# Another order of the first loads and first matmuls in a gated cross-attention and expert kernel

## The chip, the cores and the metric

The kernel runs on one core of a Trainium2 chip. The metric is the device time of one execution in microseconds. Besides the unprofiled runs there is one execution taken by the profiler; its lines give start times and durations on each engine: TensorE (PE, with its weight loads as PEld), VectorE (DVE), ScalarE (ACT), GpSimd (POOL), and SyncE (SP), which here only issues DMAs.

## What is computed

A batch of 4 sequences x of 512 tokens and width 256 attends to a context of 1601 tokens and width 192, and then goes through a layer of experts. Everything is float32.

```python
def block(x, y):                      # cross-attention, 16 heads of 16
    q = (x @ Wq + bq).reshape(B, N, 16, 16)
    k = (y @ Wk + bk).reshape(B, M, 16, 16)
    v = (y @ Wv + bv).reshape(B, M, 16, 16)
    attn = softmax(einsum("bnhd,bmhd->bhnm", q, k) / 4)
    out = einsum("bhnm,bmhd->bnhd", attn, v).reshape(B, N, 256)
    return relu(out @ W1 + b1) @ W2 + b2
x = x + tanh(g_xattn) * block(layernorm(x), ctx)
x = x + tanh(g_ffn) * experts(layernorm(x))   # one shared, two of eight routed by sigmoid scores
```

## The kernel before

**Layout.** The 16 heads are worked on in four groups of four (`G` = 4 groups, `HPG` = 4 heads), each head in 32 of the 128 partitions, of which 16 hold values. `wk_t` holds the K weights of all heads without gaps, so one product (`make_k`, lines 301 to 315) makes K of 8 heads for one of four chunks (`NCH`) of 401 or 398 context tokens; a bias row is the 97th row of the second half of the weights and meets a row of ones in the context. Each product is two matmul calls (`c` = 0, 1), and each call is two passes in float32. The result goes to PSUM, ACT copies it into `kd`, and `spread` (lines 317 to 323) then moves the rows of four heads by four DMAs, one for each head, into one of three tiles `ks` with 32 partitions a head. `make_v` (line 328) makes V of one tile of 128 context tokens (there are 13, `NKT`); it is kept in one of 15 tiles `vs`, whose unused columns hold zeros and one column of ones.

**Main loop.** The scheduler keeps the order as written for TensorE, ACT, DVE and SP. For each pair of a batch and a group, 13 steps run: in each, scores of one group (line 416, exponents on ACT at 425), the attention times V (`add_values`, 437), and already the maxima of the next group (`maximum`, 357, reduced by DVE at 368). Other work (Q, K, V of later batches, the MLP of earlier ones) is put beside given steps in the table `late` by `put`. A step that gets such work of a larger kind goes into the set `large` and does its attention-times-V product in one piece, others in two halves. A second phase, after line 697, does the experts, with pieces of the shared expert placed by `fill` between the last MLP, the last layer norm and the router.

**Start.** `first_loads` (lines 177 to 192) issues DMAs on two queues, SP's and ACT's. K weights come first on SP, then the first context chunk, x of batch 0 and the other chunks; ACT issues the K bias row, the Q bias and the V bias. Line 181 writes the bias row element by element, since the biases lie in columns in memory. A DMA is given one of eight semaphores in turn, so the issuing of a ninth waits for the first to land. ACT then packs `wk_slots` into `wk_t` (lines 660 to 665), in two copies; the second takes in the bias row. Next, in the order of lines 666 to 694: statistics of x on DVE (`stats1`), K chunks 0 and 1, the reciprocal square root of the variance by four Newton steps (`rstd_of`, lines 234 to 250), the normalised x (`apply`, line 254), its transposes (`make_xnT`), K chunks 2 and 3, the spreads for groups 0 and 1, the remaining loads (`other_loads`: gates, x of batches 1 to 3, MLP weights), Q of groups 0 and 1, and the first V tile. A loop over 13 slices then finds the maxima of group 0: four matmuls, four reductions by DVE, and one further product of V or K in each slice; the K parts of the second eight heads stand in slices 3 to 6. Three V tiles are left to the first steps of the main loop. POOL and DVE fill constant tiles at the very start (lines 157 to 166).

`rstd_of` runs on DVE for batch 0 at the start and for batch 3 at the end of attention (line 775), on POOL for the others.

Of the kernel before, what the change touches and what calls it, by code (L numbers as in the profile page):

```python
# [8 lines left out]
FP = mybir.dt.float32  # L9
AF = mybir.ActivationFunctionType  # L10
ALU = mybir.AluOpType
# [3 lines left out]
P = 128  # L15
EPS = 1e-5
HD = 16
# [8 lines left out]
def kernel(  # L26
# [43 lines left out]
    nc = tc.nc  # L70
    B, D, M = ctxT.shape
    NT, H = x.shape
    S = NT // B
# [4 lines left out]
    KC = D // 2  # L78
    NKT = -(-M // P)
    NCH = 4  # L80
    CH = -(-M // NCH)
    chunks = [(c * CH, min(CH, M - c * CH)) for c in range(NCH)]
# [44 lines left out]
    gt = const.tile([P, 2], FP, name="gt")  # L127
# [16 lines left out]
    sp1 = xattn.enter_context(tc.tile_pool(name="sp1", bufs=1, side="right"))  # L144
    esp = xattn.enter_context(tc.tile_pool(name="esp", bufs=10, side="right"))
    wq_t = sp1.tile([P, 2, G * P], FP, name="wq_t")
# [14 lines left out]
    for t in ks:  # L161
        nc.gpsimd.memset(t, 1.0)
    nc.gpsimd.memset(neg, 0.0)
    for t in vs:
        nc.gpsimd.memset(t, 0.0)
        nc.gpsimd.memset(t[:, :, HD : HD + 1], 1.0)

    def load_ctx(b, parts=((0, M),)):
        for o, n in parts:
            nc.sync.dma_start(  # L170
                out=ctx_t[:KC, :, o : o + n],
                in_=ctxT[b].rearrange("(c p) m -> p c m", p=KC)[:, :, o : o + n],
            )
# [2 lines left out]

    def first_loads():

        nc.sync.dma_start(out=wk_slots[:KC], in_=wk.rearrange("(c p) n -> p c n", p=KC))
        nc.scalar.dma_start(  # L180
            out=wk_slots[KC : KC + 1, 1, :].rearrange("o (g p) -> o g p", p=P),
            in_=bk.rearrange("(o p) g -> o g p", o=1),
        )
        load_ctx(0, chunks[:1])
        load_x(0)
        load_ctx(0, chunks[1:])
        nc.scalar.dma_start(out=bq_t, in_=bq)
        nc.scalar.dma_start(
            out=wv_t[KC : KC + 1, 1, :], in_=bv.rearrange("(o n) -> o n", o=1)
        )  # L190
        nc.sync.dma_start(out=wq_t, in_=wq.rearrange("(c p) n -> p c n", p=P))
        nc.sync.dma_start(out=wv_t[:KC], in_=wv.rearrange("(c p) n -> p c n", p=KC))

    def other_loads():
        nc.sync.dma_start(out=gt, in_=gates.partition_broadcast(P))
        for b in range(1, B):
            load_x(b)
        for h in range(NH):
            nc.sync.dma_start(
                out=w1_t[h * HD % P : h * HD % P + HD, h * HD // P, :],  # L200
                in_=w1[h * HS : h * HS + HD, :],
            )
        nc.sync.dma_start(out=b1_t, in_=b1)
        nc.sync.dma_start(out=w2_t, in_=w2.rearrange("(c p) n -> p c n", p=P))
        nc.sync.dma_start(out=b2_t, in_=b2.partition_broadcast(P))
        nc.sync.dma_start(out=rb_t, in_=rb.partition_broadcast(P))
        nc.sync.dma_start(out=ord_t, in_=order.partition_broadcast(P))
        nc.sync.dma_start(out=wr_t, in_=wrT.rearrange("(c p) e -> p c e", p=P))
# [25 lines left out]
    def rstd_of(b, mv, rstd, engine):  # L234

        var = p2.tile([P, NTB], FP, tag="var")
        nc.vector.tensor_scalar(var, mv[:, rows(b), 1], EPS, None, ALU.add)
        first = p2.tile([P, NTB], I32, tag="first")
        nc.vector.tensor_scalar(first, var.bitcast(I32), 1, None, ALU.arith_shift_right)  # L239
        nc.vector.tensor_scalar(first, first, -1.0, float(0x5F3759DF), ALU.mult, ALU.add)  # L240
        y = first.bitcast(FP)
        engine.tensor_scalar(var, var, -0.5, None, ALU.mult)  # L242
        for n in range(4):
            sq = p2.tile([P, NTB], FP, tag="sq")
            engine.tensor_tensor(sq, y, y, ALU.mult)
            engine.tensor_tensor(sq, sq, var, ALU.mult)
            engine.tensor_scalar(sq, sq, 1.5, None, ALU.add)
            to = rstd[:, rows(b)]
            engine.tensor_tensor(to, y, sq, ALU.mult)
            y = to  # L250

    xn = {}
# [1 line left out]
    def apply(b, mv, rstd, engine):  # L254
        xn[b] = p2.tile([P, NTB, H], FP, tag="xn", name=f"xn_{b}")
        for t in range(NTB):
            tt = b * NTB + t
            engine.tensor_scalar(
                xn[b][:, t, :],
                xs[b][:, t, :],  # L260
                mv[:, tt, 0:1],
                rstd[:, tt : tt + 1],
                ALU.subtract,
                ALU.mult,
            )
# [18 lines left out]
    def make_q(i, h=None, ps=None):  # L284
        b, g = divmod(i, G)
        ps = side() if ps is None else ps
        n = half_of(h)
        for c in range(2):
            nc.tensor.matmul(  # L289
                ps[:, n],  # L290
                lhsT=wq_t[:, c, g * P : (g + 1) * P],
                rhs=xnT[b][:, c, n],
                start=(c == 0),
                stop=(c == 1),
            )
        if not h:
            qT[i] = sp2.tile([P, S], FP, tag="qT", name=f"qT_{i}")
            mxs[i] = sp2.tile([P, NTB, HPG, NCH], FP, tag="mxs", name=f"mxs_{i}")
        nc.scalar.activation(qT[i][:, n], ps[:, n], AF.Identity, bias=bq_t[:, g : g + 1])  # L299

    def make_k(b, h2, part, ps=None):
        if part == 0:
            kd[b, h2] = sp1.tile([P, M], FP, tag="kd", name=f"kd_{b}_{h2}")
        o, n = chunks[part]
        ps = side() if ps is None else ps
        for c in range(2):
            r = slice(0, KC + c)
            nc.tensor.matmul(  # L308
                ps[:, :n],
                lhsT=wk_t[r, c, h2 * P : (h2 + 1) * P],  # L310
                rhs=ctx_t[r, c, o : o + n],
                start=(c == 0),
                stop=(c == 1),
            )
        nc.scalar.copy(kd[b, h2][:, o : o + n], ps[:, :n])

    def spread(i, queues=(nc.sync,)):
        b, g = divmod(i, G)
        for j in range(HPG):
            r = (g % 2 * HPG + j) * HD  # L320
            queues[j % len(queues)].dma_start(
                out=ks[i % 3][j * HS : j * HS + HD, :], in_=kd[b, g // 2][r : r + HD, :]
            )
# [222 lines left out]
    def put(where, i, kt, work, *args):  # L546
        if where is late and work not in (spread, load_ctx, load_expert, stats1, rstd_of, apply, residual):
            large.add(i * NKT + kt)
        where[i * NKT + kt].append(lambda: work(*args))
# [61 lines left out]
            for kt in range(2, NKT):  # L611
                put(late, i, kt, make_v, nb, kt)

    for kt in range(NKT - 3, NKT):
        put(late, 0, kt - (NKT - 3) - 2, make_v, 0, kt)

    def step(s):

# [32 lines left out]
    with tc.manual_schedule(  # L651
        engines={
            mybir.EngineType.PE,
            mybir.EngineType.Activation,
            mybir.EngineType.DVE,
            mybir.EngineType.SP,
        }
    ):
        first_loads()
        for c in range(2):  # L660
            r = slice(0, KC + c)
            nc.scalar.copy(
                wk_t[r, c, :].rearrange("p (h d) -> p h d", d=HD),
                wk_slots[r, c, :].rearrange("p (h d) -> p h d", d=HS)[:, :, :HD],
            )
        for t in range(NTB):
            stats1(0, t)
        for part in range(2):
            make_k(0, 0, part, ps_sc.tile([P, S], FP, tag="sc", name="k0"))
        rstd_of(0, mv1, rstd1, nc.vector)  # L670
        apply(0, mv1, rstd1, nc.vector)
        for c in range(2):
            make_xnT(0, c, ps_mx.tile([P, S], FP, tag="mx", name="xnT0"))
        for part in range(2, NCH):
            make_k(0, 0, part, ps_sc.tile([P, S], FP, tag="sc", name="k0"))
        spread(0, (nc.sync, nc.scalar))
        spread(1)
        other_loads()
        make_q(0, ps=ps_mx.tile([P, S], FP, tag="mx", name="q0"))
        make_q(1)  # L680
        make_v(0, 0)
        for u in range(NKT):
            banks = [(ps_mx, "mx") if j % 2 else (ps_sc, "sc") for j in range(HPG)]
            for bank in run([(maximum, reduce_max, (0, u), j, *banks[j]) for j in range(HPG)]):
                bank()
            if u < 3:
                make_v(0, u + 1)
            elif u < 3 + NCH:
                make_k(0, 1, u - 3)
            else:  # L690
                make_v(0, u - 3)
            if u == 3 + NCH:
                spread(2)
        nc.scalar.activation(tg, gt, AF.Tanh)
        for s in range(-2, LAST + 1):
            step(s)
    xattn.close()
# [482 lines left out]
```

## Time and profile before

| | us |
|---|---|
| runs: median (lowest to highest) of 3 | 1277.04 (1276.51 to 1277.31) |
| the profiled execution's own time | 1275.26 |
| its span (first to last instruction) | 1273.3 |
| TensorE: scores, L416 | 467.7 busy |
| TensorE: maxima, L357 (the form the page lists) | 480.8 busy |
| DVE: reductions of maxima, L368 | 479.9 busy |
| ACT: exponents, L425 | 437.7 busy |
| mean granted TensorE clock of the span | 0.996 |

A busy time counts overlapping matmuls of four row groups as one stretch in the shares, and each in a group's sum. A timeline line gives start, duration, engine, line of the code, operation, output and inputs, and in brackets the idle time of that engine just before and what ended it. A line of the chain gives start, length, engine, tile and line of work that released the next. A line of the windows gives a stretch, its width, the busy time (with the number of instructions), the granted clock, the share of DMA, and GB/s.

### The profile page before, as it was taken

What the parts mean: (1) busy time and instruction counts of PE and PEld (TensorE: products, weight loads), DVE (VectorE), ACT (ScalarE), POOL (GpSimd) and SP (SyncE); (2) the same over time, 40 slices, a digit from 0 to 9 for tenths busy, and PEclk for the clock granted to TensorE, in tenths of its full rate; (3) what the DMA queues carried; (4) which work ended last, traced back from release to release, by engine and by line L of the source; (5) the groups of instructions that cost most, each with busy time, mean ns of one, the idle gap of its engine ahead of it and who ended that gap; (6) DMA issues with size and microseconds to landing.
All of it is one profiled execution on the core that took longest, in us unless ns stands there. A gap on an engine that the chain in (4) does not pass through costs nothing.

```text
span 1273.3 us, 19722 instructions
## 1 busy us (share of the span) xinstructions
PE 1251.2 (98%) x7750; PEld 560.4 (44%) x7750; DVE 687.3 (54%) x1292; ACT 593.2 (47%) x1139; POOL 144.7 (11%) x253
## 2 busy tenths in 40 slices
PE   6999999999999999999999999999999999999998
PEld 2433334333343433334343333344256666666665
DVE  3977666666676566666656666676025511111115
ACT  2155656656555565654555556555822122222220
POOL 4000010000005000000500000020000133333320
PEclk9999999999999999999999999999999999999999
DMA  6312000002001000200010000000092011111105
GB/s 131 93 40 63 1 14 14 1 1 53 14 1 23 15 8 1 53 14 1 1 30 14 1 13 14 2 18 1 1 335 77 18 34 45 43 44 39 39 9 198
DMA packets 30992, 48.29 MB, mean 38 GB/s; under 512 B 5487, under 2 KB 21745, under 8 KB 30902
## 3 DMA queue, kind: packets, MB, share of 16 engines
q1 hardware_dynamic: 26432, 38.43, 11.5%
q0 software_dynamic: 3744, 8.40, 2.1%
q8 instruction: 62, 1.02, 0.3%
q10 hardware_dynamic: 726, 0.21, 0.1%
q14 instruction: 28, 0.23, 0.1%
HBM read 32.99 MB, written 9.31 MB: 33 GB/s over the span
## 4 chain that ended last, share of the span: by engine, by line
PE 95%; DVE 3%; DMA 1%; ACT 0%; issue 0%; SPq 0%; DVEq 0%; ACTq 0%
PE sc L416 31%; PE av L437 17%; PE gp L993 5%; PE y_ps L1011 5%; PE up L993 5%; PE mx L357 4%; PE ms L334 4%; PE ms L308 3%; PE ms L486 3%; PE ms L289 2%; PE ms L498 2%; PE up L718 2%; PE gp L718 2%; PE th L1004 1%; PE sc L357 1%; PE op L741 1%
## 5 line engine op out<-in xcount | busy, mean ns | idle before, releaser
L368 DVE TENSOR_REDUCE mxs<-mx 128x1 f32<-128x512 f32 x744 | 479.9, 685 | 250.5 <-PE mx L357 246.6
L425 ACT ACTIVATE es<-sc 128x512 f32<-128x512 f32 x804 | 437.7, 594 | 340.4 <-PE mx L357 290.8
L357 PE MATMUL mx<-ks,qT 32*128 32x512 f32 (+1 forms) x1984 | 480.8, 549 | 0.0
L416 PE MATMUL sc<-qA,ks 32*128 32x512 f32 x1608 | 467.7, 637 | 0.8 <-DVE qA L411 0.8
L416 PEld LDWEIGHTS sc<-qA,ks 32*128 32x128 f32 x1608 | 131.3, 179 | 221.5 <-issue 164.8
L437 PE MATMUL av<-es,vs 128*32 128x512 f32 (+2 forms) x1872 | 228.0, 557 | 0.1
L357 PEld LDWEIGHTS mx<-ks,qT 32*128 32x128 f32 x1984 | 164.7, 183 | 4.1 <-issue 1.9
L437 PEld LDWEIGHTS av<-es,vs 128*32 128x32 f32 (+1 forms) x1872 | 37.3, 108 | 166.9 <-issue 161.9
L1060 DVE TENSOR_TENSOR hid<-sg,up 128x512 f32<-128x512 f32 x39 | 26.8, 688 | 138.2 <-PE up L993 138.2
L242 POOL TENSOR_SCALAR var<-var 128x4 f32<-128x4 f32 x6 | 1.4, 238 | 777.8 <-DVE first L239 777.8
L1058 ACT ACTIVATE sg<-gp 128x512 f32<-128x512 f32 x39 | 23.3, 597 | 115.5 <-PE gp L993 115.5
L993 PE MATMUL gp<-w_all,xT 128*128 x156 | 73.5, 593 | 0.9 <-ACT xT L989 0.9
L1011 PE MATMUL y_ps<-w_all,hT 128*128 x312 | 73.8, 379 | 0.0
L993 PE MATMUL up<-w_all,xT 128*128 x156 | 73.4, 593 | 0.0
L334 PE MATMUL ms<-wv_t,ctx_t 96*128 96x256 f32 (+1 forms) x208 | 58.7, 404 | 0.8 <-ACT qT L299 0.8
L1011 PEld LDWEIGHTS y_ps<-w_all,hT 128*128 128x128 f32 x312 | 56.4, 190 | 6.6 <-issue 0.5
L1020 POOL DMA_INDIRECT rows_y<-y,dest x39 | 39.6, 1016 | 148.9 <-DVE y L1019 148.9
L334 PEld LDWEIGHTS ms<-wv_t,ctx_t 96*128 96x128 f32 (+1 forms) x208 | 34.5, 185 | 38.8 <-issue 23.5
L973 POOL DMA_INDIRECT xg<-rows_x,token x39 | 40.3, 1033 | 48.7 <-DVE token L957 37.1
L308 PE MATMUL ms<-ctx_t,wk_t 96*128 96x401 f32 (+3 forms) x112 | 45.2, 525 | 0.0
L1019 DVE COPY y<-y_ps 128x256 f32<-128x256 f32 x39 | 16.6, 425 | 46.2 <-PE y_ps L1011 46.2
L989 ACT COPY xT<-tx 128x256 f32<-128x256 f32 x39 | 14.6, 375 | 54.4 <-PE tx L987 54.4
(163 smaller groups left out, 982.2 us busy)
## 6 DMA issues: line engine op xcount, KB each, us to landing
ks<-kd SPq DMA_DIRECT2D x62, 100.1 KB, 3.2
w_all<-in_wgT SPq DMA_DIRECT2D x8, 512.0 KB, 9.7
w_all<-in_wuT SPq DMA_DIRECT2D x8, 512.0 KB, 10.0
w_all<-in_wdT SPq DMA_DIRECT2D x8, 512.0 KB, 10.6
w_all<-rows_y SPq DMA_DIRECT2D x8, 512.0 KB, 7.7
ctx_t<-in_ctxT SPq DMA_DIRECT2D x3, 1200.8 KB, 7.9
xb<-in_x SPq DMA_DIRECT2D x4, 512.0 KB, 5.7
rows_x<-xn SPq DMA_DIRECT2D x4, 512.0 KB, 2.8
```

The costliest lines, as they stand in the source:

```text
L308: nc.tensor.matmul(ps[:, :n], lhsT=wk_t[r, c, h2 * P : (h2 + 1) * P], rhs=ctx_t[r, c, o : o + n], start=(c == 0), stop=(c == 1),)
L334: nc.tensor.matmul(ps[:n, : NH * HD], lhsT=ctx_t[r, c, o : o + n], rhs=heads[r, c, :, :HD], start=(c == 0), stop=(c == 1),)
L357: nc.tensor.matmul(ps[:, n * REST : (n + 1) * REST] if last else ps, lhsT=qT[i][slot_of(j), qb * P : (qb + 1) * P], rhs=ks[i % 3][slot_of( ...
L368: nc.vector.tensor_reduce(mxs[i][:, qb, j, c : c + 1], ps, AX.X, ALU.max)
L416: nc.tensor.matmul(ps[:n, :], lhsT=ks[i % 3][r, o : o + n], rhs=qA[i][r, :], start=True, stop=True)
L425: nc.scalar.activation(es[(i * NKT + kt) % 2, j][:n], ps[:n], AF.Exp, scale=SCALE)
L437: nc.tensor.matmul(av[i][j * HS : (j + 1) * HS, cols], lhsT=v_of(b, kt)[:n, g * HPG + j, :], rhs=es[(i * NKT + kt) % 2, j][:n, cols], star ...
L718: nc.tensor.matmul(ps, lhsT=w_sh[:, off + c, f * P : (f + 1) * P], rhs=x2T[:, c, b * S : (b + 1) * S], start=(c == 0), stop=(c == 1),)
L973: nc.gpsimd.indirect_dma_start(out=xg[i % 4], out_offset=None, in_=rows_x, in_offset=bass.IndirectOffsetOnAxis(ap=token[:, i : i + 1], axi ...
L993: nc.tensor.matmul(ps, lhsT=xT[i][:, c, :], rhs=w_flat[:, bass.ds(owners[i] + (off + c) * I, I)], start=(c == 0), stop=(c == 1),)
L1011: nc.tensor.matmul(ps, lhsT=hT2[i][:, f, :], rhs=w_flat[:, bass.ds(owners[i] + 4 * I + f * H, H)], start=(f == 0), stop=(f == NI - 1),)
L1020: ins = nc.gpsimd.indirect_dma_start(out=rows_y, out_offset=bass.IndirectOffsetOnAxis(ap=dest[:, i : i + 1], axis=0), in_=y, in_offset=Non ...
```

## The change

It reorders the start and shortens a few pieces of it:

- Loads: K weights go first on ACT's queue, the bias row first on SP's; the first two context chunks follow there before x. Q weights move ahead of the small loads in the text, and the gates are loaded on ACT's queue in this first group.
- V tiles: only the 16 columns past the values are cleared, half of the tiles by DVE and half by POOL.
- `rstd_of`: three Newton steps for four, everywhere; on DVE two operations are fused.
- All four K chunks of the first eight heads come before the transposes of x, then their spread at once (three DMAs on SP, one on ACT), then the first K part of the other eight heads, the transposes, and Q of group 0. `kd` gets two buffers.
- In the slices: slice 0 takes Q of group 1, slices 1 to 3 the three remaining K parts, slices 4 to 12 V tiles 0 to 8. The third spread, the remaining loads and the tanh of the gates follow slice 4. V tiles 9 to 12 stand in the first four steps of the main loop, the last of them in step 1.

```diff
-    for t in vs:
-        nc.gpsimd.memset(t, 0.0)
-        nc.gpsimd.memset(t[:, :, HD : HD + 1], 1.0)
+    for n, t in enumerate(vs):
+        engine = nc.gpsimd if n % 2 else nc.vector
+        engine.memset(t[:, :, HD:], 0.0)
+        engine.memset(t[:, :, HD : HD + 1], 1.0)
...
-        nc.sync.dma_start(out=wk_slots[:KC], in_=wk.rearrange("(c p) n -> p c n", p=KC))
-        nc.scalar.dma_start(
+        nc.scalar.dma_start(out=wk_slots[:KC], in_=wk.rearrange("(c p) n -> p c n", p=KC))
+        nc.sync.dma_start(
             out=wk_slots[KC : KC + 1, 1, :].rearrange("o (g p) -> o g p", p=P),
             in_=bk.rearrange("(o p) g -> o g p", o=1),
         )
-        load_ctx(0, chunks[:1])
+        load_ctx(0, chunks[:2])
         load_x(0)
-        load_ctx(0, chunks[1:])
+        load_ctx(0, chunks[2:])
+        nc.sync.dma_start(out=wq_t, in_=wq.rearrange("(c p) n -> p c n", p=P))
         nc.scalar.dma_start(out=bq_t, in_=bq)
+        nc.scalar.dma_start(out=gt, in_=gates.partition_broadcast(P))
         nc.scalar.dma_start(
             out=wv_t[KC : KC + 1, 1, :], in_=bv.rearrange("(o n) -> o n", o=1)
         )
-        nc.sync.dma_start(out=wq_t, in_=wq.rearrange("(c p) n -> p c n", p=P))
         nc.sync.dma_start(out=wv_t[:KC], in_=wv.rearrange("(c p) n -> p c n", p=KC))
...
-        nc.sync.dma_start(out=gt, in_=gates.partition_broadcast(P))
...
-        for n in range(4):
+        for n in range(3):
...
-            engine.tensor_scalar(sq, sq, 1.5, None, ALU.add)
             to = rstd[:, rows(b)]
-            engine.tensor_tensor(to, y, sq, ALU.mult)
+            if engine is nc.vector:
+                engine.scalar_tensor_tensor(to, sq, 1.5, y, ALU.add, ALU.mult)
+            else:
+                engine.tensor_scalar(sq, sq, 1.5, None, ALU.add)
+                engine.tensor_tensor(to, y, sq, ALU.mult)
...
-            kd[b, h2] = sp1.tile([P, M], FP, tag="kd", name=f"kd_{b}_{h2}")
+            kd[b, h2] = sp1.tile([P, M], FP, tag="kd", bufs=2, name=f"kd_{b}_{h2}")
...
-    for kt in range(NKT - 3, NKT):
-        put(late, 0, kt - (NKT - 3) - 2, make_v, 0, kt)
+    for kt in range(NKT - NCH, NKT):
+        put(late, 0, kt - (NKT - NCH) - 2, make_v, 0, kt)
...
-        for part in range(2):
-            make_k(0, 0, part, ps_sc.tile([P, S], FP, tag="sc", name="k0"))
         rstd_of(0, mv1, rstd1, nc.vector)
         apply(0, mv1, rstd1, nc.vector)
+        for part in range(NCH):
+            pool, tag = (ps_mx, "mx") if part == NCH - 1 else (ps_sc, "sc")
+            make_k(0, 0, part, ps=pool.tile([P, S], FP, tag=tag, name="k0"))
+        spread(0, (nc.sync, nc.scalar, nc.sync, nc.sync))
+        make_k(0, 1, 0)
         for c in range(2):
             make_xnT(0, c, ps_mx.tile([P, S], FP, tag="mx", name="xnT0"))
-        for part in range(2, NCH):
-            make_k(0, 0, part, ps_sc.tile([P, S], FP, tag="sc", name="k0"))
-        spread(0, (nc.sync, nc.scalar))
+        make_q(0, ps=ps_sc.tile([P, S], FP, tag="sc", name="q0"))
         spread(1)
-        other_loads()
-        make_q(0, ps=ps_mx.tile([P, S], FP, tag="mx", name="q0"))
-        make_q(1)
-        make_v(0, 0)
         for u in range(NKT):
...
-            if u < 3:
-                make_v(0, u + 1)
-            elif u < 3 + NCH:
-                make_k(0, 1, u - 3)
+            if u == 0:
+                make_q(1)
+            elif u < NCH:
+                make_k(0, 1, u)
             else:
-                make_v(0, u - 3)
-            if u == 3 + NCH:
+                make_v(0, u - NCH)
+            if u == NCH:
                 spread(2)
-        nc.scalar.activation(tg, gt, AF.Tanh)
+                other_loads()
+                nc.scalar.activation(tg, gt, AF.Tanh)
```

## The prediction

> **What bounds the kernel now.** I read the page's busy rows and its chain first, then the chain in order of time at both ends, then each engine's timeline there, and last the windows for the granted clock.
>
> ```profile
> PE 1251.2 (98%) x7750; PEld 560.4 (44%) x7750; DVE 687.3 (54%) x1292; ACT 593.2 (47%) x1139; POOL 144.7 (11%) x253
> ...
> PE 95%; DVE 3%; DMA 1%; ACT 0%; issue 0%; SPq 0%; DVEq 0%; ACTq 0%
> ```
> TensorE is the bound: it idles only 22 us of 1273.3. The change removes no matmul, so it can win only where TensorE idles, runs on half clock, or sits behind DVE. The chain has two such places, the first 61 us and the stretch near 960 us. The start:
>
> ```profile
> 1.68 7.81 DMA xb<-in_x
> ...
> 9.51 0.44 DVE st L214
> ...
> 16.22 0.42 DVE xn L258
> ...
> 16.77 1.64 PE xnT L270 x8
> 18.41 4.38 PE k L308 x8
> 22.80 1.72 PE q L289 x4
> 24.52 1.73 PE ms L289 x4
> ```
> x lands at 9.5, DVE normalises until 16.6, and only then does TensorE go on. What it could have done meanwhile, the K weights hold back:
>
> ```profile
> 7.34 1.68 PE L308 MATMUL k<-ctx_t,wk_t 96*128 96x401 f32 x2 [7.34 <-DMA ctx_t<-in_ctxT]
> 10.92 4.28 PE L308 MATMUL k<-ctx_t,wk_t 97*128 97x401 f32 x6 [1.91 <-ACT wk_t L662]
> 16.77 0.30 PE L270 MATMUL xnT<-ident,xn 128*128 128x128 f32 x1 [1.57 <-DVE xn L258]
> ```
> ```profile
> 10.46 0.41 ACT L662 COPY wk_t<-wk_slots 97x256 f32<-97x256 f32 x1 [4.20 <-DMA wk_slots<-in_bk]
> ```
> TensorE's timeline, then one line of ACT's: start, duration, and in brackets the idle time before and what ended it. The bias row (2 KB, issued at 0.75 on ACT's queue) lands at 10.43, later than context and x. TensorE idles 7.34 + 1.91 + 1.57 us, and 0.78 at 26.2. The end of attention:
>
> ```profile
> 965.46 1.29 PE L270 MATMUL ms<-ident,xn 128*128 128x128 f32 x4 [1.62 <-DVE xn L258]
> ```
> ```profile
> 14.98:18.39 3.41, 1.84 (x10) 1.00 0.18 43
> 18.39:21.80 3.41, 3.41 (x7) 0.50 0.00 0
> 963.88:967.29 3.41, 1.83 (x6) 1.00 0.00 0
> 967.29:970.71 3.42, 3.42 (x8) 0.50 0.43 153
> ```
> First the same wait for xn in the last layer norm; then windows (width, TensorE busy, granted clock). After 3.41 us of which 1.6 are idle, the next 3.41 run at half clock, each time.
>
> **Start, inputs.** From 3 to 9 us the windows show about 240 GB/s, so order decides. Before, summed at that rate from 1.5 us, wk would end at 3.1, chunk 0 at 4.4, x at 6.6; they landed at 5.15, 7.2, 9.48: 2 to 2.9 later. After: wk leads ACT's queue, SP's has the bias row, chunks 0 and 1, x, chunks 2, 3, then wq. The bias row has 512 packets of 4 bytes. In bursts the trace serves 145 in half a us, on 4 to 5 engines: 0.016 us each, 32 per engine, 0.5 us. Sum: wk 3.1, row 3.65, chunk 0 4.9, chunk 1 6.2, x 8.4, chunk 2 9.7, chunk 3 11.0; with 2.2 of lag: 7.1, 8.4, 10.6, 12.0, 13.2. Bounds for x: 9.5 (as before, the trickle gone) and 12.
>
> [...] The row in the trace says where the 9.7 us went: 360 of its packets were through by 6.0 us, the rest trickled until 9.5 one by one beside x's packets. At the head of SP's own queue it has no x beside it. I take about 5 us.
>
> ACT: wk issue 0.4, bq 0.4 to 2.0, gates 0.6 (new there), bv 0.4, table 1.28, wk_t copies 2 x 0.41: done by 6.3, hidden behind chunk 0 at 7.1.
>
> **Start, K.** Cold matmuls start 0.667 us apart, warm ones 0.337. With windows as in this trace the clock comes at 11.57: 6.6 cold matmuls from 7.1, the other 9.4 of parts 0 to 3 warm, 14.8 (chunk 3 at 13.2 just keeps up). Copy to kd until 15.5. The spread of kd into ks: before, its fourth transfer, the second on ACT, landed at 29.2, 5.9 us after the copy (a maximum starts at 29.30 on it); now three go through SP and one through ACT, and the DMA view has SP's at 3.4 to 5.1 from their issue; I take 5.5 from the copy: 21.0. Bounds 4.8 and 6.5.
>
> **Start, Q.** DVE from x to the last xn took 8.12. Newton falls from 4 x 4 to 3 x 3 instructions, 7 x 0.20 = 1.4 less (the fused one, not in this trace at that size, priced as a 128x32 one of its kind at 0.18): x at 10.6, last xn 17.3. TensorE does the first K part of the second heads meanwhile (4 x 0.337, 14.8 to 16.2), before xn is there, so it costs nothing; if xn came by 15 it would cost its 1.35. Transposes, two copies, q, bias: before 17.60 to 25.7 with K between; without it 0.45 + 1.1 + 1.3 + 0.7, so qT at 20.8. Maxima start at 20.9 instead of 28.07, the fourth at 21.0.
>
> **Start, slices.** DVE reduces 4 x 0.60 = 2.39 us a slice; slices with V are DVE's, those with K TensorE's (2.61). Before, slice 1's first reduction starts at 32.54 and the last ends at 61.26. After: fourth maximum 21.0 + 1.1 (29.30 to 30.4 before), q1 1.73, from a slice's first maximum to its first reduction 1.16 (28.07 to 29.23): slice 1 at 25.0. Then three K slices 7.83, eight 19.12, the short one 1.42: 53.4. Gain 61.26 - 53.4 = 7.9. One V more falls into step 1 of the main loop: step 0 with a V took 4.15 (69.16 to 73.31), step 1 without 3.56, so 0.6 back. Net 7.3.
>
> **Edits at nothing.** Eight V tiles cleared on DVE, each 256 elements (by the 1601 in 1.39 us: 0.22, plus 0.1 for the ones): 3 us, or 5.6 at twice that, between 2.5 and x; beyond it they would delay xn. They cannot gain: DVE waits for x. POOL's shorter clearing ends before 10 instead of 13.7; nobody waits for it by 15. POOL's three Newton steps: batches 1 to 3 have slack, nobody waits on these rows. A second kd buffer frees ACT of a 2.4 us wait. SP's queue: chunk 2 now waits for wk, chunk 3 for the row, wq for chunk 0, wv for bq; behind them stand the spreads, due only at 15.5. The other 25 loads (15.7 us of issue from 28.15) move behind the third spread, to about 33 to 49; x of batch 1 is used near 90. Tanh moves up and has no table load at its line.
>
> **End of attention.** The last layer norm is on DVE too: 7 x 0.20 = 1.4 off the 1.62 wait. The half-clock window follows it. [...] The rows fall after a window 54% busy, while 25.22 to 28.63, busy 2.63 (77%), keeps the clock. With 0.2 idle left I take the row: 3.41 us at half clock is 1.7 us of work, say 1.6. Bounds 0 and 1.7. Sum 3.0. What follows shifts whole: TensorE is continuous there, and the router's chain starts from its matmuls.
>
> **Rivals.**
> *Clock windows fall elsewhere.* TensorE will idle about 1 us before the maxima; with the pauses around it one window near 17 to 24 may fall below what keeps the clock, 1.7 us lost; or the window at 967 stays, 1.6 lost. For: both dips of this trace. Against: 77% busy was kept. Gain 7 to 8.7: 1268.4 to 1270.1.
>
> *The bias row still lands at 10.4.* Then K part 0 ends its second half after 10.9 as before, the clock comes about 15, K ends near 18.2, the fourth spread lands at 24.4: 3.4 later. Gain 10.3 - 3.4 = 6.9: 1270.1. For: its 9.7 us in the trace. Against: the bursts.
>
> *Slower: the row blocks SP's queue.* If each 4-byte packet costs much more at the head, chunk 0 and x stand behind 32 of them per engine. The row's whole 9.7 us divided by 32 is 0.30 us at most, which puts x near 16 to 17 and the maxima near 27: still about 5 won, 1272. From about 0.36 an element (x at 21, maxima at 31.4) the 3.0 of the end is eaten; at 0.6, 20 us of row, it is 1282.
>
> **How the numbers follow.** The profiled execution took 1275.26 (span 1273.3 and 1.96 around it), 1.78 under the median of the runs shown. 1275.26 - 7.3 - 3.0 = 1265.0, or 1266.8 against the median 1277.04. Forecast 0.58 (1264.2 to 1268.4: x and spread bounds of about 1.5 either way); clock 0.20; late row 0.13; the queue blocked 0.09, of which 0.04 slower and 0.05 nothing measurable. A difference under 0.2% (2.6 us) cannot be told from none. Range 1264.2 to 1271.2. Faster 0.91, same 0.05, slower 0.04.
>
> **What would show it.** Right: wk_t's second copy ends before 7; matmuls of K follow one another from about 7 to 15; maxima near 21; slice 1's reductions from 25; the wait for the last xn near 0.2; a full clock after it. Wrong: the second wk_t copy still waiting for the row, x after 12, a half-clock window in the slices, or the wait for xn replaced by another.

## The result, and the profile after

| | before | after |
|---|---|---|
| runs: median (lowest to highest) of 4 each | 1277.17 (1276.51 to 1277.76) us | 1268.01 (1266.34 to 1268.65) us |
| ratio after to before, 95% interval | | 0.9926 (0.9909 to 0.9944) |
| the profiled execution's own time (span) | 1275.26 (1273.3) | 1266.34 (1264.5) |

The kernel is faster by 0.74%, 9.2 us in the medians and 8.9 in the profiled executions. The changed kernel run again beside the experiments gave 1266.75 (1265.97 to 1269.04), ratio 0.9929 (0.9915 to 0.9942). The forecast was 1266.8.

First the page of the kernel after: busy time of each engine, and the shares of the chain that ended last.

```profile
PE 1246.0 (99%) x7742; PEld 558.7 (44%) x7742; DVE 686.9 (54%) x1294; ACT 592.6 (47%) x1139; POOL 133.7 (11%) x213
...
PE 95%; DVE 2%; DMA 1%; issue 1%; ACT 0%; SPq 0%; DVEq 0%; ACTq 0%
```

DVE and ACT are as busy as before; POOL has 11 us less, in 40 instructions fewer (16 of clearing, 24 of Newton steps). TensorE's idle time fell from 22 to 18.5 us, and its busy time by 5.2 us. Some 4.3 of these are work that no longer runs on half clock (an estimate: the two windows of 3.41 us shown above are gone, which is 3.4, and ahead of the clock TensorE is busy for 3.9 us instead of 5.7, half of which is 0.9). Now TensorE's timeline at the start:

```profile
7.91 7.54 PE L312 MATMUL k<-ctx_t,wk_t 96*128 96x401 f32 x16 [7.91 <-DMA ctx_t<-in_ctxT]
15.29 1.51 PE L312 MATMUL ms<-ctx_t,wk_t 96*128 96x401 f32 x4
16.64 1.04 PE L274 MATMUL xnT<-ident,xn 128*128 128x128 f32 x8
17.91 1.98 PE L293 MATMUL q<-xnT,wq_t 128*128 128x512 f32 x4 [0.24 <-ACT xnT L277]
20.68 0.69 PE L361 MATMUL sc<-ks,qT 32*128 32x512 f32 x1 [0.78 <-ACT qT L303]
```

All K of the first eight heads is one unbroken row of 16 matmul instructions (eight calls of two passes), from 7.91 to 15.45 us. The waits of 1.91 us for the bias row and of 1.57 us for xn are gone; 0.24 and 0.78 are left. The clock comes at 11.77 us (14.98 before), and no window at half clock follows until the end of the span. The windows on both sides of 11.77 (stretch, width, TensorE busy, granted clock, DMA share, GB/s):

```profile
8.36:11.77 3.41, 3.41 (x6) 1.00 1.09 266
11.77:15.19 3.42, 3.42 (x11) 1.00 1.02 247
```

The trace has no record of the clock ahead of 11.77, and the view prints 1.00 there too. What shows the half clock is the matmuls: six in the first window, eleven in the next; those of K start 0.667 us apart before 11.77 and 0.337 after it. "The clock comes" means this place in every trace below. Why K no longer waits shows in ACT's timeline, in the copy of K weights that takes in the bias row:

```profile
6.84 0.41 ACT L666 COPY wk_t<-wk_slots 97x256 f32<-97x256 f32 x1 [1.47 <-DMA wk_slots<-in_bk]
```

It starts at 6.84 instead of 10.46, before context chunk 0 is there. DVE's timeline has the first reduction of slice 1, which was at 32.54:

```profile
25.97 0.69 DVE L372 TENSOR_REDUCE mxs<-sc 128x1 f32<-128x512 f32 x1 [1.65 <-PE mx L361]
```

The last reduction of group 0 ends at 54.38 instead of 61.26. At the end of attention, TensorE's timeline:

```profile
957.90 1.29 PE L274 MATMUL ms<-ident,xn 128*128 128x128 f32 x4 [0.22 <-DVE xn L262]
```

And the windows of the kernel after, one from the start and the one in which that wait falls (stretch, width, TensorE busy, granted clock, DMA share, GB/s):

```profile
18.60:22.01 3.41, 2.63 (x11) 0.89 (x10) 0.18 (x1) 0.69 (x1) 0.00 (x0) 1.00 0.97 145
957.40:960.82 3.42, 3.20 (x10) 1.37 (x10) 1.41 (x4) 1.19 (x2) 1.84 (x7) 1.00 0.33 118
```

(This form of the view gives the other engines' busy time too, in the order PE, PEld, DVE, ACT, POOL, ahead of the clock.) The wait fell from 1.62 to 0.22 us, the window is busy for 3.20 us of 3.42, and the clock after it stays full.

From these starts the gain can be summed. The start won 6.9 us (61.26 to 54.38). By the transposes of 957.90 the lead is 7.56 (965.46 before), of which 1.40 is the shorter wait there: so 0.7 was given back on the way, in the main loop. From the transposes to a later product of TensorE, the first of `whose` (line 941 before, 943 after), it took 28.13 us before (until 993.59) and 26.45 after (until 984.35): 1.68 is the window at half clock. Together 6.88 - 0.72 + 1.40 + 1.68 = 9.24. The spans differ by 8.8. The lead of 9.24 holds until the last load of the experts' rows; the chain there, before and then after:

```profile
1252.28 8.99 DMA w_all<-rows_y
```
```profile
1243.20 9.36 DMA w_all<-rows_y
```

Its issue starts 9.24 earlier (1241.00 for 1250.24), but it lands only 8.72 earlier (1252.56 for 1261.28). About 0.5 is lost in this load; why it took longer is not known.

### The profile page after: what moved, and what is told of

Read it like the earlier page. It is cut to its first block, busy times and chain, and to the rows that moved or that the text cites. A ratio compares the mean times of both kernels' runs of the same rounds, so it can differ in the third digit from the quotient of the medians.

```text
span 1264.5 us, 19650 instructions
## 1 busy us (share of the span) xinstructions
PE 1246.0 (99%) x7742; PEld 558.7 (44%) x7742; DVE 686.9 (54%) x1294; ACT 592.6 (47%) x1139; POOL 133.7 (11%) x213
## 4 chain that ended last, share of the span: by engine, by line
PE 95%; DVE 2%; DMA 1%; issue 1%; ACT 0%; SPq 0%; DVEq 0%; ACTq 0%
PE sc L420 32%; PE av L441 17%; PE gp L995 5%; PE y_ps L1013 5%; PE up L995 5%; PE mx L361 4%; PE ms L338 4%; PE ms L312 3%; PE ms L490 3%; PE ms L293 3%; PE ms L502 2%; PE up L720 2%; PE gp L720 1%; PE th L1006 1%; PE sc L361 1%; PE op L743 1%
```

## The experiments

My theory was the prediction's own. The rivals: one part of the change does it all (the loads, or the Newton steps); DVE's new clearing work or the row at the head of SP's queue takes something back. The runs of the kernel before beside the three groups of experiments had medians of 1276.45 (17 runs), 1276.57 (9) and 1276.45 (9), so the groups can be compared with each other.

### The loads as before

```diff
 (the changed kernel, with first_loads of the kernel before)
-        nc.scalar.dma_start(out=wk_slots[:KC], ...)   # bias row on nc.sync
+        nc.sync.dma_start(out=wk_slots[:KC], ...)     # bias row on nc.scalar
-        load_ctx(0, chunks[:2]); load_x(0); load_ctx(0, chunks[2:])
+        load_ctx(0, chunks[:1]); load_x(0); load_ctx(0, chunks[1:])
 (and the gates in other_loads again)
```

> The changed kernel with the load order of before (gates back among the later loads, too). Theory (order of matmuls and order of loads both needed): the second half of K part 0 waits for the bias row until about 10.9 us again, K of the first heads ends near 18, the first reduction of slice 1 comes at 28.5 to 29.5 instead of 25.97, and the time lies 2.5 to 3.5 us over the changed kernel's, with the whole gain at the end of attention kept. Rival (the order of the matmuls is all of it): slice 1 within 0.5 us of 25.97 and the time within 0.5 us of the changed kernel's.

1271.09 us (1269.36 to 1273.45), ratio 0.9953 (0.9939 to 0.9966). Slice 1 came at 28.78. But the kernel has a second loss that neither theory named. ACT's timeline, then TensorE's:

```profile
42.71 0.20 ACT L696 ACTIVATE tg<-gt 128x2 f32<-128x2 f32 x1 [4.63 <-DMA gt<-in_gates]
```
```profile
43.23 1.39 PE L338 MATMUL ms<-wv_t,ctx_t 96*128 96x256 f32 x4 [1.75 <-ACT vs L345]
```

The tanh after slice 4 waits 4.63 us for gates that are now loaded late, behind it stands ACT's copy of a V tile, and behind that TensorE; the window around it (40.55 to 43.96) is busy for 1.66 us, and the next two run at half clock (until 50.79). So moving the tanh into the slices rests on the early load of the gates. The next kernel leaves that loss out.

```diff
 (as above, but the gates stay early)
         nc.scalar.dma_start(out=bq_t, in_=bq)
+        nc.scalar.dma_start(out=gt, in_=gates.partition_broadcast(P))
```

> As the first experiment, but with the gates on ACT's queue from the start, as in the changed kernel: in the first experiment ACT's tanh stood in the slices waiting for gates that were loaded behind the third spread, and held TensorE for some 1.7 us and the clock for two windows. Theory: slice 1's first reduction at 28 to 29 again (2 to 3 us later than in the changed kernel), and now the same distance at the end of the slices: 2 to 3 us over the changed kernel, 1269 to 1270. Rival (order of matmuls is all): within 0.7 of it.

1269.66 us (1269.42 to 1270.15), ratio 0.9944 (0.9931 to 0.9958): 2.9 above the repeat of the changed kernel, 1.65 above its first series. TensorE's timeline shows the row holding K again:

```profile
7.38 1.68 PE L312 MATMUL k<-ctx_t,wk_t 96*128 96x401 f32 x2 [7.38 <-DMA ctx_t<-in_ctxT]
10.00 8.15 PE L312 MATMUL k<-ctx_t,wk_t 97*128 97x401 f32 x14 [0.94 <-ACT wk_t L666]
```

The second half of K part 0 starts at 10.00, K ends at 18.15, 2.7 later, and slice 1 is at 28.75, 2.8 later. Most of that is not the wait itself. The pause of 0.94 us leaves TensorE busy for only 3.03 us of the window from 9.61 to 13.03, and the clock comes at 16.44 instead of 11.77; 4.7 us more at half clock cost 2.3 (an estimate from the two spacings). This is what the rival "the bias row still lands at 10.4" described; it was costed at 3.4.

### The loads alone, in the kernel before

```diff
 (the kernel before, with first_loads of the changed kernel; the gates move with it)
```

> The kernel before with the new load order alone. Theory: in the old order of matmuls x is the gate, and x now lands at about 10.7 instead of 9.5, so the first transposes come about 1.2 us later; K parts 0 and 1 run earlier, into time that was idle anyway. No gain: 1275.5 to 1279, slice 1's first reduction between 31.5 and 34. Rival (the late bias row is what cost): slice 1 at about 29.5, 3 us faster than before.

1276.88 us (1274.0 to 1278.41, 13 runs), ratio 0.9998 (0.9989 to 1.0008): nothing; slice 1 at 32.98, as expected. TensorE's timeline says why:

```profile
17.74 1.57 PE L270 MATMUL xnT<-ident,xn 128*128 128x128 f32 x5 [3.86 <-DVE xn L258]
```

In the old order of matmuls K parts 0 and 1 end at 13.9, and then TensorE waits 3.86 us for xn, because x now lands 1.3 later (DVE's first statistics at 10.79 instead of 9.51). What the row no longer costs, x costs. The new load order pays only with the matmul order that has four K parts to do before x. In the profiled execution of this kernel the wait of 1.62 at the end of attention was there, but no window at half clock followed:

```profile
963.00:966.40 3.40, 1.78 (x5) 1.00 0.00 0
966.40:969.80 3.40, 3.40 (x13) 1.00 0.43 154
```

Nine of the thirteen runs had a mean clock of 0.995 or 0.996 and took 1276.4 to 1278.41; the other four, with the profiled execution among them, had 0.999 and took 1274.0 to 1276.05. What clock the nine lost is in no trace, so the "nothing" is that of the medians, with the clock in it.

### The Newton steps alone, and without them

```diff
 (the kernel before)
-        for n in range(4):
+        for n in range(3):
 (and the fused last operation on DVE)
```

> The kernel before with three fused Newton steps alone (three for four on POOL too). Theory: 1.4 us at the start, where the chain runs through DVE, and 1.4 at the end of attention, and the half-clock windows after both waits go with them, 1.7 each: 3 to 6.2 us faster, 1271 to 1274. [...] Second rival (the start is bound by loads, not by DVE): 1.4 to 3.

1272.43 us (1271.54 to 1273.65), ratio 0.9966 (0.9952 to 0.9979): 4.0 won in the medians, where the loads alone gave nothing; 3.4 in the profiled executions. Nearly all of it is at the end: the transposes start at 963.97 (1.5 earlier), and the product `whose` at 990.41 (3.2 earlier), as the wait is 0.22 and no window falls. At the start the same edit won 0.1. DVE's timeline there, and POOL's:

```profile
11.96 1.61 DVE L237 TENSOR_SCALAR var<-mv 128x4 f32<-128x4 f32 x1
13.60 0.17 DVE L239 TENSOR_SCALAR first<-var 128x4 int32<-128x4 int32 x1
```
```profile
12.95 0.52 POOL L165 MEMSET vs<- 128x512 f32 x1
```

An operation on 4 numbers a partition, 0.17 us elsewhere, takes 1.61 us, and ends within 0.1 us of the end of POOL's last full-size clearing. This I had not expected, and it gave a further experiment (below).

```diff
 (the changed kernel, with rstd_of of the kernel before)
```

> The changed kernel with the four unfused Newton steps of before. Theory: the wait for xn at the end of attention is 1.6 again and a half-clock window follows it: 3.0 more. At the start xn comes 1.4 later, of which 0.3 to 1.3 is seen, since the fourth spread transfer lands at 21.9 anyway. In all 3.3 to 4.5 over the changed kernel. Rival: only the waits return, no window: 1.7 to 2.7 over it.

1270.01 us (1268.5 to 1271.82), ratio 0.9946 (0.9933 to 0.996); its profiled execution took 3.67 more than the changed kernel's. Slice 1 is 0.8 later; the rest is the end of attention. TensorE's timeline and the windows:

```profile
960.07 1.29 PE L271 MATMUL ms<-ident,xn 128*128 128x128 f32 x4 [1.61 <-DVE xn L259]
```
```profile
958.62:962.03 3.41, 1.96 (x6) 0.97 (x7) 2.18 (x9) 1.05 (x2) 1.84 (x7) 1.00 0.03 10
962.03:965.44 3.41, 3.41 (x8) 1.75 (x7) 1.19 (x4) 0.57 (x1) 0.55 (x2) 0.50 0.41 144
```

With four steps the wait is back at 1.61, and the window at half clock with it. The product `whose` is 3.85 later than in the changed kernel: 0.8 from the start (where the clock also came 1.4 later, at 13.13), 1.4 from the wait, 1.7 from the window.

### Newton steps and clearing together

```diff
 (the kernel before with the three Newton steps, and)
-    for t in vs:
-        nc.gpsimd.memset(t, 0.0)
+    for n, t in enumerate(vs):
+        engine = nc.gpsimd if n % 2 else nc.vector
+        engine.memset(t[:, :, HD:], 0.0)
```

> The kernel before with three fused Newton steps and with the V tiles' clearing halved and split between DVE and POOL. Theory: with the Newton steps alone the first small DVE operation took 1.61 us while POOL cleared, which ate the 1.4 us at the start; without POOL clearing at that time it takes 0.17, xn comes 1.2 to 1.6 us earlier than in that kernel, the transposes with it as far as K parts 0 and 1 let them (they end near 15), 0.5 to 1.3 us at slice 1, time 1271 to 1272. Rival (the long operation has another cause): it takes over 0.4 again and slice 1 stays at 32.4.

1270.92 us (1269.66 to 1272.24), ratio 0.9952 (0.9939 to 0.9966). DVE's timeline has the same operation again:

```profile
11.74 0.17 DVE L238 TENSOR_SCALAR var<-mv 128x4 f32<-128x4 f32 x1
```

POOL's clearing is over at 8.05, the operation is at 0.17, the first xn comes 1.64 earlier than with the Newton steps alone, and slice 1 is at 29.28 instead of 32.45. Of these 3.2 us 1.64 are the earlier xn; the other 1.5 are the clock, which came at 16.66 instead of 21.42, so that K chunks 2 and 3 took 2.86 us instead of 4.38. How much of the earlier clock is due to the clearing is not shown. By the end less is kept: the medians differ by 1.5, with intervals that overlap, and the profiled execution has a window at half clock in its main loop, though TensorE was busy throughout the window ahead of it:

```profile
873.41:876.82 3.41, 3.41 (x32) 1.00 0.00 0
876.82:880.23 3.41, 3.41 (x20) 0.50 0.00 0
```

In the kernel with the Newton steps alone, then, POOL's clearing took back most of what they had saved at the start. Whether it matters in the changed kernel is the next question.

```diff
 (the changed kernel, with the V tiles cleared whole on POOL)
-    for n, t in enumerate(vs):
-        engine = nc.gpsimd if n % 2 else nc.vector
-        engine.memset(t[:, :, HD:], 0.0)
-        engine.memset(t[:, :, HD : HD + 1], 1.0)
+    for t in vs:
+        nc.gpsimd.memset(t, 0.0)
+        nc.gpsimd.memset(t[:, :, HD : HD + 1], 1.0)
```

> The changed kernel, with the V tiles cleared whole and by POOL alone, as before. In the kernel with three Newton steps alone, DVE's first small operations after the statistics took 1.6 us instead of 0.17 while POOL was still clearing. Theory: POOL's clearing slows DVE's small operations, so the normalised x comes 0.5 to 1.5 us later and slice 1 0.3 to 1.3 later: up to 1.3 us slower. Rival (the forecast: nobody waits for POOL): xn within 0.2 us of the changed kernel's when measured from the landing of x, no difference in time.

1267.22 us (1265.51 to 1269.49), ratio 0.9921 (0.9908 to 0.9935): no difference, so the expectation failed. In the profiled execution x came late (first statistics at 11.15), DVE's small operations began at 13.41, when POOL was nearly through, and took 0.17 each. Longer ones were seen in kernels whose x came earlier (first statistics at 9.51, 9.69 and 10.79), so that they met more of the clearing; here the two hardly meet. So in the changed kernel the smaller clearing is harmless, and a gain from it is not measured there. This run does have a window at half clock in the slices (24.56 to 27.97, after one that was busy for 2.64 us), with slice 1 at 28.97.

### The changed kernel again, and the row in one piece

> The changed kernel once more, unaltered, for more runs of it. Its profiled execution had no half-clock window after the start and took 1266.3; its other runs took 1267.9 to 1268.7 at a mean clock a little lower. Theory: the windows run free of the program, so these runs lose one or two, 1.7 us each, where TensorE pauses: median 1267 to 1268.5. Rival (the first run was an outlier of another kind): clocks as high as in the profile and still 1268.

1266.75 us, given above; slice 1 at 25.78 in its profiled execution, which again has no window at half clock after the start.

```diff
-        nc.sync.dma_start(
-            out=wk_slots[KC : KC + 1, 1, :].rearrange("o (g p) -> o g p", p=P),
-            in_=bk.rearrange("(o p) g -> o g p", o=1),
-        )
+        nc.scalar.dma_start(
+            out=bk_row[KC : KC + 1, :], in_=bk.rearrange("(o p) g -> o (p g)", o=1)
+        )
 (ACT then picks the columns with four copies of 1x64 into wk_t)
```

> The changed kernel, but the bias row comes as one piece of 2 KB on ACT's queue behind the K weights, in memory order, and ACT picks the columns with four copies of 64 elements. Theory: the element-wise row at the head of SP's queue left the engines nearly idle from 3.3 to 4.8 us and held up the issue of the second chunk; without it chunk 0 lands about 1.2 us earlier (near 6.5), x near 9.5, slice 1's first reduction at 24.7 to 25.2 instead of 25.97, the time 0.7 to 1.3 under the changed kernel's. Rival (the bandwidth was not lost, only the order differs; ACT's extra copies then stand before K): slice 1 at 25.8 or later.

1267.51 us (1265.29 to 1267.76), ratio 0.9922 (0.9908 to 0.9936): not to be told from the changed kernel. Yet the loads are much earlier. The windows of the changed kernel, then those of this one:

```profile
3.00:4.00 1.00, 0.00 (x0) 0.00 (x0) 1.00 (x7) 1.00 (x1) 1.00 (x2) 1.00 0.66 129
4.00:5.00 1.00, 0.00 (x0) 0.00 (x0) 1.00 (x8) 0.28 (x2) 1.00 (x2) 1.00 0.57 59
```
```profile
3.00:4.00 1.00, 0.00 (x0) 0.00 (x0) 1.00 (x7) 0.91 (x1) 1.00 (x2) 1.00 0.99 338
4.00:5.00 1.00, 0.00 (x0) 0.00 (x0) 1.00 (x8) 0.38 (x1) 1.00 (x2) 1.00 1.08 297
...
19.97:23.38 3.41, 2.75 (x9) 1.12 (x10) 1.59 (x3) 0.60 (x1) 0.00 (x0) 1.00 0.71 98
23.38:26.79 3.41, 3.41 (x8) 1.19 (x10) 0.89 (x2) 0.51 (x1) 0.00 (x0) 0.50 0.00 0
```

With the row element by element at the head of SP's queue, 129 and 59 GB/s pass from 3 to 5 us (last column); in one piece 338 and 297. This run changes the form of the row and its queue together; which of the two does it is not separated. K starts 1.5 us earlier (6.43) and x is 2.0 earlier (8.72). But the clock came only at 13.14 in this execution:

```profile
6.31:9.73 3.42, 3.29 (x5) 1.00 1.19 292
9.73:13.14 3.41, 3.41 (x6) 1.00 0.91 260
```

K started 0.12 us into the first of these windows, and the clock rose only after the next, which was busy throughout. So K ended at 15.4, as in the changed kernel. The slices then lost 1.7 us to a window at half clock, and slice 1 came at 27.63, where 24.7 to 25.2 was expected. So the row's price is shown in the loads, while what it costs the kernel is at most what the run-to-run scatter hides.

### The K part behind Q

```diff
-        make_k(0, 1, 0)
         for c in range(2):
             make_xnT(0, c, ...)
         make_q(0, ...)
+        make_k(0, 1, 0)
```

> The changed kernel, with the first K part of the second heads moved behind Q of group 0, into the wait for qT. Theory: slice 1 hangs on the fourth spread transfer (its matmul starts at 21.87) and not on qT, so slice 1's first reduction stays within 0.2 us of 25.97 and the time within 0.4. Rival (qT is the bound): qT about 0.8 us earlier and slice 1 with it, 25.2.

The kernel that ran has the row in one piece as well, so the expectation, which speaks of the changed kernel alone, does not fit it. 1266.12 us (1265.19 to 1267.55), ratio 0.992 (0.9907 to 0.9934); the clock came at 10.85, K ended at 14.1, and slice 1 was at 24.69. The same edit by itself:

> The changed kernel with only the first K part of the second heads moved behind Q of group 0; the earlier run of that move also carried the bias row in one piece, so it did not test it alone. Theory: slice 1 hangs on the fourth spread transfer, so slice 1's first reduction stays within 0.3 us of 25.8 to 26 (for a clock that comes near 11.7; a later clock adds up to 1.3) and the time within 0.5 of the changed kernel's 1266.8. Rival (qT is the bound): slice 1 0.8 us earlier.

1266.73 us (1266.13 to 1268.46), ratio 0.9924 (0.991 to 0.9937); slice 1 at 25.95, the fourth maximum at 21.86, both within 0.02 of the changed kernel's first profile. The K part ahead of the transposes costs nothing, because the fourth maximum waits for its spread anyway: in seven traces (the changed kernel twice, with four Newton steps, with the clearing on POOL, with the row in one piece, with this move, and with both) it starts 6.42 to 6.48 us after K ends, wherever that is (14.1 to 16.8). That is what the prediction said of it. The run with both moves differs from this one by the row alone: its slice 1 is 1.26 earlier, with a clock 1.0 earlier, and its median 0.6 lower, within the scatter.

### A clock that is up before K

```diff
 (the row in one piece, the K part behind Q, and after first_loads:)
+        for n in range(10):
+            nc.tensor.matmul(wp[:, :P], lhsT=warm, rhs=warm, start=True, stop=True)
 (warm: a 128x128 tile of zeros)
```

> The kernel with the bias row in one piece and the K part behind Q, and ten matmuls on a zero tile at the very start on TensorE (their result goes nowhere), from about 1.7 to 6 us, while it has nothing else to do. Theory: K parts run cold because the clock comes only after a full window of activity; with the ten the clock comes at 5 to 9 instead of 10.9 to 14.3, K of the first heads ends near 12.6 instead of 14.1 to 15.5, slice 1 at 23.3 to 24.2 instead of 24.7 (or 27.6), time 1264 to 1265.5. Rival (loads bound K, chunk 3 lands last): K ends at 13.5 or later, gain under 0.5 over the same kernel without them (1266.1).

1265.5 us (1265.16 to 1268.9), ratio 0.9917 (0.9901 to 0.9933). TensorE's timeline and the windows:

```profile
1.06 4.63 PE L669 MATMUL wp<-warm 128*128 128x128 f32 x20 [1.06 <-DVE warm L158]
6.53 6.11 PE L315 MATMUL k<-ctx_t,wk_t 96*128 96x401 f32 x16 [0.83 <-ACT wk_t L672]
13.74 1.64 PE L277 MATMUL xnT<-ident,xn 128*128 128x128 f32 x8 [1.11 <-DVE xn L265]
15.62 3.46 PE L296 MATMUL q<-xnT,wq_t 128*128 128x512 f32 x4 [0.24 <-ACT xnT L280]
```
```profile
12.57:15.98 3.41, 2.07 (x10) 1.24 (x10) 1.86 (x7) 1.49 (x3) 0.00 (x0) 1.00 0.65 112
15.98:19.40 3.42, 3.42 (x5) 1.35 (x4) 0.00 (x0) 0.36 (x2) 0.00 (x0) 0.50 0.96 148
```

The clock was up at 5.74 and K ended at 12.64, as expected. Then TensorE waited 1.11 us for xn and 0.24 for the transposes' copy, the window fell, and Q took 3.46 us instead of 1.98. Slice 1 came at 24.72, no better than the run before it (24.69). The bound had become x. This is the lowest median of all, 0.5 under the lowest run of the changed kernel (1265.97), but its own runs go up to 1268.9 and the intervals of the two ratios overlap, so I do not call it faster.

## Why the prediction was right

The mechanisms were right, and so was the size within its range: 10.3 us forecast, 8.9 in the profiled executions, 9.2 and 9.8 in the medians. The first series, 1268.0 us, lies just inside the 1264.2 to 1268.4 of the main case.

**Start.** Forecast 7.9 at the last reduction, measured 6.9. The term that was mis-sized is the loading order. The row was to land at about 5 us and chunk 0 at 7.1; the row's copy started at 6.84 and chunk 0 let K start at 7.91. By the sum's own lag of 2.2 us the row would have been due at 5.9, not 5. I had priced it at 0.5 us of all queues; its packets took from 3.3 to 4.3, and the copy that waits for it started 2.5 us after them. Still, the row came 3.6 us earlier than on ACT's queue in the kernel before (its copy at 6.84 for 10.46). What I had left out is what the row does to the queue behind it. SP's timeline in the changed kernel:

```profile
1.64 2.68 SPq L171 DMA_DIRECT2D ctx_t<-in_ctxT  x2
4.36 0.45 SPq L105 DMA_DIRECT2D xb<-in_x  x1
```

The issue of two context chunks took 2.68 us, so x was issued only at 4.36; with the row in one piece the two take 0.88, and x comes 2.0 earlier. This is the slower rival at a small scale, not the 0.36 us an element from which it would decide. Against the forecast x was not late (first statistics at 10.72, x forecast at 10.6). K's start was, by 0.8, and most of that stays: K's end 15.45 for 14.8, the fourth maximum 21.87 for 21.0; with 1.92 us for Q of group 1 instead of 1.73, slice 1 comes at 25.97 for 25.0. From there to the last reduction it took 28.4 us, as forecast. Two things went better than the sum. The last xn came at 16.75 for 17.3, because the 8.12 us that I took over from the kernel before held 0.7 us of stretched operations (below). And the clock came at 11.77, where I had taken 11.57 from the windows of the trace before: that was luck, for in the variants with the new loads it came anywhere from 10.85 to 14.32, and at 14.32 K ended at 16.78.

**Given back.** Forecast 0.6 for one more V tile in step 1, measured 0.7 between 54 and 958 us, of which 0.6 at that step: the first exponents on ACT lead by 6.88 (59.30 for 66.19), those after step 1 by 6.25 (71.71 for 77.96).

**End of attention.** Forecast 1.4 and 1.6, measured 1.40 and 1.68. The four-step version of the changed kernel brings both back. The second is not certain, though: in the kernel with the loads alone the same wait was followed by a full clock.

**The steps that were wrong** did not move the verdict. "POOL's shorter clearing ends before 10 instead of 13.7; nobody waits for it by 15": its end was right (8.05), but in the kernel before DVE's operations are longer beside it. There, three small operations after 12 us take 0.48, 0.48 and 0.41 us instead of 0.17 (one of them below), with the Newton steps alone one takes 1.61, with the loads alone one 0.51; in the traces in which POOL is through before them, and in the one in which it is nearly so, all take 0.16 or 0.17. The view I read, waits by semaphore, cannot show this: the time is inside the operation. DVE's timeline of the kernel before:

```profile
12.01 0.48 DVE L239 TENSOR_SCALAR first<-var 128x4 int32<-128x4 int32 x1
```

It ends at 12.49, 0.03 us after the end of one of POOL's clearings of 0.52 us (11.94 to 12.46). The 1.61, from 11.96 to 13.57, is longer than one such clearing and spans three of them (they start at 11.93, 12.44 and 12.95). What holds the operation back beside them no trace shows.

"77% busy was kept" as a bound for the clock: the window of 2.63 us busy in the changed kernel kept it, but one of 2.64 and one of 2.75 us (81%) lost it in two experiments. TensorE's busy time in a window, as the profile has it, does not settle it. So the rival "clock windows fall elsewhere", given 0.20, seems real in single executions: the three runs of the changed kernel at a mean clock of 1.0 took 1266.0 to 1266.8, five of the six at 0.998 to 0.999 took 1267.9 to 1269.0 (the sixth 1266.2). Where they lost it is in no trace.

**Which part gives how much.** As a ladder of medians, in this one order: before 1276.5; Newton steps 1272.4; with the clearing 1270.9; with the matmul order and the slices 1269.7; with the load order 1266.8 to 1268.0. In another order the shares are others: the load order alone was worth nothing in the kernel before, and the clearing nothing measurable in the kernel after. The first rung is shown at its place, the last by slice 1's start (28.75 to 25.97); the 1.5 and 1.2 of the middle are near what five runs can tell.

**Left open.** Why the last load took 0.5 us longer; what makes the clock fall, for the busy share does not settle it.

## What to carry to other kernels

Where the bound engine waits, ask also what its clock does after the wait: a shortened chain of small operations on another engine returned its 1.4 us and, against executions in which a window had fallen, 1.7 more in clock. The earlier loads were worth nothing in the old matmul order (ratio 0.9998) and 1.65 to 2.9 us in the new one, which had work for them, so judge a load order and a matmul order together. And look for stretched durations, not only for waits: an operation of 0.17 us took 1.61 here, and no view of waits lists the difference.

## What the runs showed of the hardware that was not expected

- Beside POOL's fills, `tensor_scalar` operations of DVE on 128x4 elements took 0.41 to 0.51 us (0.48, 0.48 and 0.41 in the kernel before, 0.51 with the loads alone) and once 1.61 (with the Newton steps alone); with POOL done at 8.05, in the changed kernel, the same operations took 0.16 and 0.17. Two others beside the fills of the kernel before took 0.20 and 0.17, and the `tensor_tensor` operations right after the long ones, while POOL was still filling, kept their 0.16.
- With a row of 512 elements of 4 bytes at the head of a queue, 129 and 59 GB/s pass in the two microseconds from 3 to 5 us (338 and 297 with the row in one piece on the other queue), though its own packets take 9 ns each and end at 4.3 us.
- In the changed kernel and its variants with the bias row early (all but the one with matmuls on zeros), the clock comes between 10.85 and 14.32 us. In thirteen of the fourteen traces it comes at the end of the first window in which TensorE was busy for 3.40 us or more (in the one with the matmuls on zeros, for 3.37); windows busy for 3.29 us (with the row in one piece) and 3.03 (with the old loads and the gates early) did not bring it. In the run with the row in one piece 0.12 us at the start of a window thus went with the loss of a whole one. The edges of the windows do not lie at one place from the kernel's start: counted back in steps of 3.41 us from where the clock comes, the first lies at 1.34 us in the kernel before, 1.54 in the changed one, 0.68 with the clearing on POOL, 2.91 with the row in one piece, and 0.62 with that and the K part behind Q (an estimate from the clock's 14.98, 11.77, 14.32, 13.14 and 10.85).
- Apart from the end of the span, a fall to half clock lasts 3.41 us, once two such windows (43.96 to 50.79 with the old loads). It fell after windows of 1.66, 1.83, 1.84, 1.96, 2.07, 2.64 and 2.75 us busy, and stayed after one of 1.78, after others of 2.63 and 2.70, and near the end of six traces after 1.6 to 2.0. After 3.20 us busy at the end of attention no fall was seen. And in the main loops of three kernels it fell after a window that was busy throughout. All three of these windows hold the router's 16 matmuls of only 8 columns each, 1.95 us of the busy time; another window that holds them, 970.71 to 974.12 in the kernel before, was followed by a full clock. So in these three no pause of TensorE stood ahead of the fall, and the busy time that the profile shows does not settle it.
